# A four-layer graph network on one core: block-ordered loads and stores in fewer transfers, and another order of the first weight loads

## The chip, the cores and the metric

The kernel runs on one core of a Trainium2 chip. The metric is the time of one execution on the device in microseconds (us). Three runs of the kernel before took 5391.73, 5395.11 and 5400.12 us.

The engines are TensorE (PE in the profile, with its weight loads as PEld), VectorE (DVE), ScalarE (ACT), GpSimd (POOL), and SyncE (SP), which here does nothing but issue transfers (DMAs). ACT can issue transfers too.

## What is computed

There are 128 samples. Each is a graph of 128 nodes with 512 features (`x`, 128 x 128 x 512) and a weighted adjacency matrix (`adj`, 128 x 128 x 128). Four layers follow each other, each of the form `x = layernorm(x + layer(x, adj))`, all in float32:

```
# layer 0: attention-weighted diffusion with K = 3 hops
Xw = X @ Wv + bv;  e = leaky_relu(sj[:, None, :] + si[:, :, None] + ab)    # sj, si = Xw @ aw halves
transition = A * exp(e) / sum(A * exp(e));  H = sum_k (Xk @ Wk[k] + bk[k]),  X_{k+1} = transition @ Xk;  relu(H)
# layer 1: two hypergraph convolutions, H = (adj != 0), with relu and layer norm between them
out = D^-1 H B^-1 H^T (x @ W^T) + b                                       # 512 -> 1024, then 1024 -> 512
# layer 2
A = exp(leaky(8 * tanh((s + s^T) / 8))) * adj, rows normalised and rescaled;  out = A @ x @ w
# layer 3: 8-head attention whose scores are multiplied by 2 * adj;  softmax, context, output projection
```

In layer 1 the product `H B^-1 H^T` is one 128 x 128 matrix per sample, called K in the kernel. It is used in both convolutions.

## The kernel before, in words

**Tiling.** Samples go in pairs (`U = 2`), and two pairs go through a layer's stages together. A tile of kind `four` holds a pair's 2 x 512 features for 128 nodes (512 KB); `sq` holds a pair's 128 x 128 matrices (128 KB). All matrix products with weights are done by Strassen's scheme, in layers 0 and 1 and for the attention's q and k twice nested (`twice`, L842; `strassen`, L630). For this the weight blocks and their differences are made once (`prepare0`, L894, for layer 0; the `park_` functions for the later layers, which leave them in DRAM until `take_` brings them in), and sums of blocks of the turned x are made on POOL (`lefts`, L805; `operands`, L615).

**Block order.** A product needs x with features on the partitions. [...] So tiles that are to be turned are loaded in an order of blocks (`from_dram`, L776, for x and adj from the inputs), or go through DRAM and come back in it (`through_dram`, L755). Each of these transfers fills 32 of the 128 partitions, so four make a whole tile. `from_dram` issues four for each sample of a pair: eight transfers of 64 KB for x (runs of 512 bytes), eight of 16 KB for adj (runs of 128 bytes). `turned` (L788) then does the transpose of a tile in one DVE instruction.

`through_dram` has two forms. With `in_order=True` it stores in four transfers, one for each 32 partitions, so that after load and transpose the rows stand in their natural order. With `in_order=False` it stores in one transfer; the rows then come back permuted (row `4 r + m` at place `32 m + r`), and whoever uses them has to undo that. The hidden rows `h` of layer 1 use the first form, with 128 KB per transfer; each sample of a pair is stored by itself.

**Layer 1 around K** (`layer1`, L1172). A pair's adj comes by `from_dram`, is turned, compared with zero on DVE and scaled on POOL. PE multiplies mask and scaled mask into K ("bank<-sq,sq" in the profile). ACT copies K out of PSUM, SP stores it to DRAM in one transfer, and much later, before the second convolution, SP loads it again in one transfer of 130 KB.

**The start** (`prepare0`). The three weights wk of layer 0 (1 MB each) are staged in tiles of `first`. ACT's queue fetches the first column half of all three by row chunks, in loads of 64 KB, and the small vectors (`aw`, `bv`, `bk`, `ab`; those of `aw` and `bv` are read four bytes at a time). The rest comes by SP, after or between the loads of wv (128 KB each) and the first x. ACT then copies the parts into W's blocks, and DVE and POOL form the differences (`combine`, L514; `combine_apart`, L509; `combine_once_more`, L520). DVE also forms `Wv @ aw` by dots of wv's rows with a broadcast `aw` ("junk"); two columns of the blocks B11 and B21 hold the result, so the first products wait for them.

**What sets the order.** All instructions are first recorded in `Plan` (L174) with a key (the stage's place in time, from tables such as `WHEN0`, `WHEN1`, `WHENT`) and with their dependencies. Then `Plan.order` (L239) places them on the five engines one by one, by estimated costs, free buffers and free time; `Plan.deadlines` (L359) gives due times from a first pass, and `Plan.emit` (L370) keeps the best of a few passes and issues everything in that order. Instructions under `plan.together()` stay next to each other. Transfers go round eight semaphore lanes: the ninth waits until the first has landed. [...] Since there is one planner for everything, a change of a few instructions moves others on all engines.

All instructions pass through one line (L381), so the profile tells groups apart by tile names, not by lines. "first" is the large area for the weights of layer 0 and later ones; "bank" and "t" are PSUM; "e" is layer 0's transition matrix on its way through DRAM; "x1d" is x after layer 0.

## Time and profile before

| | |
|---|---|
| median of three runs | 5395.11 us |
| the profiled execution | 5396.67 us |
| its span in the trace | 5394.1 us |
| PE busy in the span | 5308.3 us |
| granted PE clock, mean | 0.996 |
| moved by DMA | 813.71 MB, 151 GB/s |
| transfers issued by SP | 4378, most of them 0.43 us each |

Layer 0 runs from the start to about 1350 us, layer 1 to about 3105 us, layers 2 and 3 to the end. In the rows of groups "x6044 | 1766.2, 434" is the number of instructions, their busy time in us and the mean of one in ns. A product in float32 is two PE instructions. In waits, "16.7, 11, 12.7" is the sum in us, how many, and the longest; the name behind the arrow is what ended the wait by the trace. In a timeline, the first number is the start, the second the length, and several like instructions are merged.

### The profile page before, as it was taken

To read this page: it belongs to the slowest core of one execution; us is meant where nothing else is said; L and a number is where in the kernel's file an instruction comes from. 1 tells how busy PE (TensorE), PEld (TensorE's weight loads), DVE (VectorE), ACT (ScalarE), POOL (GpSimd) and SP (SyncE) were. 2 spreads that over 40 slices of the span, in tenths; PEclk is the share of its full clock that TensorE was granted. 3 is DMA by queue.
4 is the path that set the end of the run, shared out by engine and by line. 5 is a ranking of instruction groups with operands and counts; after the bars stand their busy time and mean duration, and the time that the engine had idled before them with its cause. 6 is when DMAs were issued, how large, how long until landed. Compare 5 with 4: busy or idle time off the path is not lost.

```text
span 5394.1 us, 93993 instructions
## 1 busy us (share of the span) xinstructions
PE 5308.3 (98%) x29039; PEld 4233.2 (78%) x29039; DVE 4436.2 (82%) x11721; ACT 2403.0 (45%) x6085; POOL 3902.7 (72%) x4937
## 2 busy tenths in 40 slices
PE   8999999999999999999999999999999999999998
PEld 4555555555788888888888889888998898888988
DVE  6788888887888888888888878878888888888876
ACT  3334344343444444444444444444444444444444
POOL 6777787675766767676766577777877777778776
PEclk9999999999999999999999999999999999999999
DMA  3444444435554545454554745554555455555543
GB/s 103 133 145 127 143 144 129 132 112 186 147 156 144 161 147 157 148 156 148 156 154 143 246 135 167 154 165 151 164 156 161 153 164 156 163 152 161 160 148 111
DMA packets 842414, 813.71 MB, mean 151 GB/s; under 512 B 269612, under 2 KB 642868, under 8 KB 841912
## 3 DMA queue, kind: packets, MB, share of 16 engines
q1 hardware_dynamic: 838914, 806.65, 49.2%
q8 instruction: 231, 3.78, 0.3%
q14 instruction: 271, 2.22, 0.1%
q10 hardware_dynamic: 2998, 1.06, 0.1%
HBM read 458.38 MB, written 349.04 MB: 150 GB/s over the span
## 4 chain that ended last, share of the span: by engine, by line
PE 88%; DVE 7%; issue 2%; DMA 1%; ACT 1%; POOL 1%; SPq 0%; ACTq 0%; DVEq 0%; POOLq 0%
PE bank L381 69%; PE t L381 20%; DVE out L381 1%; DVE four L381 1%; DVE first L381 1%; DVE col L381 1%; DVE junk L381 1%; SPq L381 0%; DVE side L381 0%; ACT out L381 0%; POOL four L381 0%; DMA four<-x1d 0%; POOL first L381 0%; ACT four L381 0%; DVE rows L381 0%
## 5 line engine op out<-in xcount | busy, mean ns | idle before, releaser
L381 PE MATMUL bank<-first,four 128*128 128x386 f32 (+2 forms) x6044 | 1766.2, 434 | 30.9 <-DVE four L381 15.8
L381 PEld LDWEIGHTS bank<-first,four 128*128 128x128 f32 (+1 forms) x6044 | 1098.5, 190 | 608.8 <-issue 107.7
L381 DVE TENSOR_TENSOR out<-bank,out 128x386 f32<-128x386 f32 (+1 forms) x1999 | 969.9, 504 | 245.3 <-PE bank L381 178.9
L381 POOL TENSOR_TENSOR out<-out 128x772 f32<-128x772 f32 (+2 forms) x262 | 359.1, 1380 | 265.9 <-DVE out L381 188.6
L381 POOL TENSOR_TENSOR four<-four 128x256 f32<-128x256 f32 (+2 forms) x484 | 391.6, 823 | 212.9 <-DVE four L381 153.3
L381 DVE TENSOR_TENSOR four<-bank,four 128x256 f32<-128x256 f32 x1025 | 421.6, 418 | 131.8 <-PE bank L381 122.6
L381 PE MATMUL bank<-first,out 128*128 128x256 f32 x1850 | 458.6, 380 | 1.2 <-DVE four L381 0.6
L381 POOL TENSOR_TENSOR col<-col,neghalf 128x2 f32<-128x2 f32 x320 | 228.8, 715 | 310.9 <-DVE col L381 310.5
L381 ACT COPY out<-bank 128x258 f32<-128x258 f32 (+2 forms) x510 | 204.6, 404 | 544.8 <-PE bank L381 387.9
L381 POOL TENSOR_TENSOR four<-four,four 128x256 f32<-128x256 f32 (+2 forms) x514 | 432.2, 849 | 12.8 <-DVE four L381 5.2
L381 PEld LDWEIGHTS bank<-first,out 128*128 128x128 f32 x1850 | 345.2, 190 | 62.3 <-issue 10.5
L381 ACT ACTIVATE four<-four,col,col 128x512 f32<-128x512 f32 (+1 forms) x314 | 279.6, 914 | 138.7 <-POOL col L381 132.5
L381 DVE TENSOR_TENSOR first<-bank,first 128x256 f32<-128x256 f32 (+1 forms) x601 | 242.7, 416 | 104.4 <-PE bank L381 90.3
L381 PE MATMUL bank<-four,first 128*128 128x128 f32 (+3 forms) x1848 | 292.6, 302 | 1.7 <-DVE out L381 0.9
L381 DVE BATCH_NORM_STATS2 col<-four 128x6 f32<-128x512 f32 x392 | 260.3, 679 | 9.3 <-ACT four L381 8.7
L381 PE MATMUL t<-out,sq 128*128 128x512 f32 x512 | 258.9, 600 | 2.9 <-DVE sq L381 2.5
L381 PEld LDWEIGHTS bank<-four,first 128*128 128x128 f32 (+2 forms) x1848 | 241.7, 186 | 20.1 <-DVE out L381 2.8
L381 PE MATMUL bank<-first 128*128 128x128 f32 (+1 forms) x1972 | 256.0, 277 | 1.5 <-DVE out L381 1.1
L381 PE MATMUL bank<-out,first 128*128 128x128 f32 (+2 forms) x1524 | 251.8, 307 | 4.2 <-ACT side L381 2.2
L381 PEld LDWEIGHTS bank<-first 128*128 128x128 f32 (+1 forms) x1972 | 231.6, 182 | 15.8 <-issue 5.8
L381 PE MATMUL t<-first,four 128*128 128x256 f32 (+2 forms) x1052 | 237.9, 356 | 2.5 <-DVE four L381 1.2
L381 PEld LDWEIGHTS bank<-out,first 128*128 128x128 f32 (+1 forms) x1524 | 207.5, 185 | 27.6 <-issue 8.1
(532 smaller groups left out, 12891.5 us busy)
## 6 DMA issues: line engine op xcount, KB each, us to landing
h<-four SPq DMA_DIRECT2D x312, 128.0 KB, 2.5
four<-in_x_dram SPq DMA_DIRECT2D x504, 64.0 KB, 2.0
four<-in_x_dram SPq DMA_DIRECT2D x61, 512.0 KB, 4.5
x1d<-four SPq DMA_DIRECT2D x61, 512.0 KB, 2.9
out<-x1d SPq DMA_DIRECT2D x51, 512.0 KB, 4.6
first<-S SPq DMA_DIRECT2D x51, 512.0 KB, 4.3
out<-h SPq DMA_DIRECT2D x50, 512.0 KB, 5.3
four<-x1d SPq DMA_DIRECT2D x48, 512.0 KB, 5.2
```

Source lines behind the costliest of these rows:

```text
L381: call(*map(real, args), **{n: real(a) for n, a in kw.items()})
```

## The change

`from_dram` fills 32 partitions for both samples of a pair with one transfer, so four instead of eight per tile: 128 KB each for x and 32 KB for adj. The tile then holds sample j's blocks behind those of sample j - 1, and a new `turned_two` writes the transpose through a pattern with one more dimension. The rows of h are stored with `in_order=False`, in one transfer of 512 KB each. Because they come back permuted, K is loaded again in four transfers that read every fourth row. In `prepare0` wk comes in column halves with all row chunks, in loads of 128 KB: the first halves on ACT's queue, with the small vectors next to the last one, the second halves on SP.

```diff
     def from_dram(src, kind):
 
-        nj, _, n = src.shape
-        t = kind().rearrange("p u f -> p (u f)").rearrange("p (m j w) -> p m j w", m=4, j=nj)
-        for j in range(nj):
-            with plan.together():
-                for k in range(4):
-                    sp.dma_start(t[k * Q:(k + 1) * Q, :, j],
-                                 src[j].rearrange("(m r) (k w) -> k r m w", r=Q, k=4)[k],
-                                 run=n // 4, parts=Q)
-        return t.rearrange("p m j w -> p (m j w)")
+        nj, rows_, n = src.shape
+        w = n // 4
+        t = kind().rearrange("p u f -> p (u f)").rearrange("p (m w) -> p m w", m=4 * nj)
+        with plan.together():
+            for k in range(4):
+                sp.dma_start(t[k * Q:(k + 1) * Q], bass.AP(tensor=src.tensor, offset=src.offset + k * w,
+                                                           ap=[[n, Q], [Q * n, 4 * nj], [1, w]]), run=w, parts=Q)
+        return t.rearrange("p m w -> p (m w)")
...
+    def turned_two(dst, t):
+
+        ve.transpose(dst.rearrange("p (j q) (m r) -> p j m q r", j=U, r=Q),
+                     t.rearrange("p (j m q a) -> p j m q a", j=U, m=4, a=Q))
...
-        def fetch_part(queue, m, chunks, half):
-            at = chunks, slice(half * h, half * h + h)
-            fetch(queue, stage[m][:, at[0], at[1]], wk0[m], *at, h)
...
+        def fetch_half(queue, m, half):
+            columns = slice(half * h, half * h + h)
+            fetch(queue, stage[m][:, :, columns], wk0[m], slice(0, 4), columns, h)
...
-        for m in range(3):
-            fetch_part(ac, m, low, 0)
         awc, bvc = fixed(2 * C, name="aw_c"), fixed(C, name="bv_c")
         ab_b, bk0b = fixed(1, name="ab_b"), row()
-        with plan.together():
-            for c, v, n in ((awc, aw, 2 * C), (bvc, bv0, C)):
-                ac.dma_start(c, bass.AP(tensor=v.tensor, offset=v.offset, ap=[[1, P], [P, n]]), run=1)
-            ac.dma_start(bk0b[:3], bk0, parts=3)
-            ac.dma_start(ab_b, rows(ab, 1), run=1)
         for m in range(3):
-            fetch_part(sp if m else ac, m, high, 0)
+            with plan.together():
+                fetch_half(ac, m, 0)
+                if m == 2:
+                    for c, v, n in ((awc, aw, 2 * C), (bvc, bv0, C)):
+                        ac.dma_start(c, bass.AP(tensor=v.tensor, offset=v.offset, ap=[[1, P], [P, n]]), run=1)
+                    ac.dma_start(bk0b[:3], bk0, parts=3)
+                    ac.dma_start(ab_b, rows(ab, 1), run=1)
...
         plan.key = WHEN0[0] + .05
         for m in range(3):
-            fetch_part(sp, m, every, 1)
+            with plan.together():
+                fetch_half(sp, m, 1)
...
-            turned(xT[-1].rearrange("p u c n -> p (u c) n"), xb)
+            turned_two(xT[-1].rearrange("p u c n -> p (u c) n"), xb)
...
-            turned(AT, ab)
+            turned_two(AT, ab)
...
-            kept.append(part(scratch(f"K{i}", P, U * M), lambda t: t, 0))
-            sp.dma_start(kept[-1], K.rearrange("p b n -> p (b n)"), run=U * M)
+            d = scratch(f"K{i}", P, U * M)
+            kept.append(lambda m, d=d: part(d, lambda t: t.rearrange("(r m) n -> m r n", m=4)[m], 0))
+            sp.dma_start(part(d, lambda t: t, 0), K.rearrange("p b n -> p (b n)"), run=U * M)
...
-                loads.append(through_dram(h[r][b].rearrange("p (j g) (k w) -> p j (g k) w", j=1, k=2), f"h{i + b}"))
+                loads.append(through_dram(h[r][b].rearrange("p (j g) (k w) -> p j (g k) w", j=1, k=2), f"h{i + b}", False))
...
-            sp.dma_start(K.rearrange("p b n -> p (b n)"), kept[r], run=U * M)
+            with plan.together():
+                for m in range(4):
+                    sp.dma_start(K[m * Q:(m + 1) * Q].rearrange("p b n -> p (b n)"), kept[r](m), run=U * M, parts=Q)
```

More of the change, by code (lines that the diff above doesn't have):

```diff
@@ L903, in fetch @@
         def fetch(queue, dst, src, chunks, columns, run):
-            with plan.together():
-                for k in range(4):
-                    queue.dma_start(dst[k * Q:(k + 1) * Q],
-                                    src.rearrange("(k c a) f -> k a c f", k=4, a=Q)[k][:, chunks, columns],
-                                    run=run, parts=Q)
-        def fetch_part(queue, m, chunks, half):
-            at = chunks, slice(half * h, half * h + h)
-            fetch(queue, stage[m][:, at[0], at[1]], wk0[m], *at, h)
@@ L914, in prepare0 @@
-        low, high, every = slice(0, 2), slice(2, 4), slice(0, 4)
-        st = [four() for _ in range(2)]
-        for g, chunks in enumerate((low, high)):
-            plan.key = -9.7 + .2 * g
-            fetch(sp, st[g], wv0, chunks, slice(0, D), D)
+            for k in range(4):
+                queue.dma_start(dst[k * Q:(k + 1) * Q],
+                                src.rearrange("(k c a) f -> k a c f", k=4, a=Q)[k][:, chunks, columns],
+                                run=run, parts=Q)
+        def fetch_half(queue, m, half):
+            columns = slice(half * h, half * h + h)
+            fetch(queue, stage[m][:, :, columns], wk0[m], slice(0, 4), columns, h)
@@ L919, in prepare0 @@
+        st = [four() for _ in range(2)]
+        for g in range(2):
+            plan.key = -9.7 + .2 * g
+            with plan.together():
+                fetch(sp, st[g], wv0, slice(2 * g, 2 * g + 2), slice(0, D), D)
         plan.key = -9
-        for m in range(3):
-            fetch_part(ac, m, low, 0)
         awc, bvc = fixed(2 * C, name="aw_c"), fixed(C, name="bv_c")
         ab_b, bk0b = fixed(1, name="ab_b"), row()
-        with plan.together():
-            for c, v, n in ((awc, aw, 2 * C), (bvc, bv0, C)):
-                ac.dma_start(c, bass.AP(tensor=v.tensor, offset=v.offset, ap=[[1, P], [P, n]]), run=1)
-            ac.dma_start(bk0b[:3], bk0, parts=3)
-            ac.dma_start(ab_b, rows(ab, 1), run=1)
```

## The prediction, made before the changed kernel ran

> **What bounds the kernel now.** I read the page's first part first, then the busy time by stretches of 135 us, then the waits of TensorE (PE) in the stretches that stand out.

> ```profile
> PE 5308.3 (98%) x29039; PEld 4233.2 (78%) x29039; DVE 4436.2 (82%) x11721; ACT 2403.0 (45%) x6085; POOL 3902.7 (72%) x4937
> ...
> 0.00:135.00 135.00, 111.25 (x295) 56.64 (x296) 94.33 (x223) 48.06 (x108) 86.47 (x107) 0.94 0.39 103
> 135.00:270.00 135.00, 134.14 (x408) 72.81 (x407) 105.54 (x274) 53.39 (x120) 100.40 (x123) 1.00 0.45 133
> ...
> 1215.00:1350.00 135.00, 123.64 (x396) 69.46 (x394) 97.99 (x278) 49.72 (x109) 73.23 (x95) 0.96 0.57 186
> 1350.00:1485.00 135.00, 130.05 (x620) 108.04 (x621) 115.31 (x329) 66.76 (x110) 95.30 (x140) 0.97 0.50 145
> ...
> 5265.00:5400.00 135.00, 115.73 (x861) 103.07 (x860) 85.63 (x213) 60.77 (x205) 84.20 (x95) 0.96 0.31 102
> ```

> The columns are the stretch, its length, then the busy time of PE, weight loads, DVE, ACT and POOL, the granted clock, the DMA share and GB/s. PE is busy 5308 of 5394 us. Of the 86 us in which it idles, 24 lie in the first stretch, 11 + 5 around 1350 (where layer 0 ends and layer 1 begins), 13 in the last 129 us. A stretch in the middle of a layer loses 0.3 to 1 us. So nothing that shortens DMA or SP work in mid-layer can pay; only the start, the change of layer and the tail can.

> ```profile
> PE bank L381 <- DVE four L381: 12.7, 1, 12.7
> ...
> PE bank L381 <- POOL sq L381: 10.0, 1, 10.0
> PE t L381 <- DVE sq L381: 2.5, 1, 2.5
> ```

> The first line is the first 60 us: PE waits for the turned x. The other two are 1200 to 1400: one wait of 10 us for a mask operand, one of 2.5 us for a turned transition matrix. What SP issued before each:

> ```profile
> 14.21 4.45 SPq L381 DMA_DIRECT2D first<-in_L_gnn_Wk_dram  x8
> 18.70 3.74 SPq L381 DMA_DIRECT2D four<-in_x_dram  x8
> 22.49 5.65 SPq L381 DMA_DIRECT2D first<-in_L_gnn_Wk_dram  x12
> ...
> 1339.22 4.70 SPq L381 DMA_DIRECT2D e<-sq  x8
> 1343.97 3.75 SPq L381 DMA_DIRECT2D sq<-in_adj_dram  x8
> ```

> SP issues back to back, one transfer per 0.47 us, from 14 to 28 us. At 1343.97 it issues the adj load that the 10 us wait is for, behind eight stores of e.

> [...] the clock is 0.50 from 40 to 50 us, and after the 10 us wait four t products take 3.43 us where they take 1.88. So each long wait costs more than its length. [...] Here the x blocks of 64 KB land in 2.0 us and the wv loads of 128 KB in 2.8, so 128 KB per issue moves more per issue. [...] The row of 128x1024 transposes shows 1236 ns.

> **The change, part by part.**

> (1) Fewer issues. Loads of x go from 8 to 4 per pair (64 pairs, -256), adj blocks likewise (-256), h stores from 8 to 2 per pair (-384), K loads from 1 to 4 (+192), wk on SP from 20 to 12 (-8): -712 of 4378. At 0.43 us that is 306 us less of SP's queue. Bytes and run lengths stay. In mid-layer this hides under PE: worth 0. The h store's one issue saves about 3 x 0.43 us before its reload, also under PE. K's last piece is issued 3 x 0.43 = 1.3 us later, and in the trace nobody waited for K's load: 0.

> (2) Transposes. Same elements, same 32-element runs, but a pattern with one more dimension (2x4x4x32 for 4x8x32). Not in the trace. From below: no reason for a gain. From above: twice the time, 64 x 1.24 = 79 us of DVE in layer 0 and 64 x 0.43 = 28 in layer 1. I take 0[...].

> (3) The start. In the changed built order SP issues x of the first pair (4), wv (8), x of the second pair (4), then the 12 second halves of wk. The last of these is place 27 of the queue; it was 45. That is 18 x 0.47 = 8.5 us of issue, but the bytes do not shrink: 0.5 + 1.0 + 0.5 + 1.5 MB on SP and 1.5 MB on ACT's queue are 5.0 MB. At 218 GB/s (the stretch from 5 to 10 us) they need 23 us from 2.9, so they land near 26 where the old last half was issued at 28.1 and landed near 31. PE's first product does not come earlier. It needs whole column halves of all three wk (3.0 MB with x and wv, landing at about 15 to 16.7), then ACT's copies, then on DVE one subtraction (0.56), the transpose (1.24) and four dots (4 x 0.76 = 3.0, with the read of the accumulator), then ACT's small copy: about 22 to 24, against 22.44. On ACT's queue the 4-byte loads of aw and bv now stand behind four wk loads; whatever they delay is in that span. What does come earlier is the second pair's transpose, at 31.92 before. In the changed order, from DVE's first subtraction (16.5 to 18.4) to that transpose stand 4 subtractions, 1 transpose, 8 dots, 3 short adds and 2 more subtractions, 6 x 0.56 + 1.24 + 8 x 0.76 + 3 x 0.28 = 11.5 us: 28 to 30. POOL's sums, and the combinations for wk's second half (POOL at 40.6 before), follow it 2 to 4 us earlier. I take **-3 us** for the start; both ends are +3 (wk's halves late) and -8 (a half-clock stretch at 40 to 50 goes too).

> (4) The change of layer. Idle at 1325 to 1385: 0.62 + 0.52 + 2.54 + 10.05 + 0.74 + 0.46 + 0.46 = 15.4 us. Half clock after the two long waits: (3.78 - 1.88) + (1.06 - 0.59) + (1.38 - 0.61) + (3.43 - 1.88) = 4.7. Sum 20.1. In the changed order the third pair's adj load is whole (4 issues), right behind the reload of an e, ahead of the seven w2 loads and of the last e stores; before, half of it stood behind them. I put it at about 1318. Landing takes 5 us under the weight loads (DMA share 1.0 there), then DVE and POOL 5 us each, so the operand stands at 1328 to 1332. PE reaches that product after 15.6 us of listed work from the first mask product (1311.7), near 1327.6. A wait of up to 5 us, with half clock up to 2.3, remains; the 2.8 us of short waits stay. The last e is then queued on SP behind the third K store, hence behind this product: e stores 1333.9 to 1337.6, fourth adj load to 1339.5, both usable by 1344 to 1350; PE has 41 rows of products (18 us) to do in between and wants them at 1350. What is late next is thus this pair, with little to spare. Gain 20.1 - 5 - 2.3 - 2.8 = **-10 us**; ends 0 (the wait only moves) and -17.

> (5) Everything else is reordered, since one planner places all instructions. PE's mid-layer idle is 0.3 to 1 us in 135; I take 0, with +-3. The tail keeps its order in kind: 0.

> Sum: -3 - 10 = -13. The profiled execution took 5396.67 us for its span of 5394.1, and it is 1.6 above the median of the three runs; on the median, 5395.11 - 13 = 5382.

> **Rivals.**

> (A) The wait moves. The last e, its adj load and the third K store are one chain on SP; if the third product is late by more than the 6 us of slack above, PE stops at the e product instead, and the start's gain is all that stays: 5395 - 3 = 5392. For it: POOL is busy 8.3 of 10 us at 1340 to 1350, so sums may be late anyway. Against it: 41 rows stand in between where there were 11.

> (B) The transposes cost more, on the slower side. Place: DVE in layer 0, busy about 113 of 135 us. Price: up to 79 us of DVE, of which a half would delay the adds that PE waits for: 39, less the 13 gained, so about 5421. It decides from the point where more than 24 us are not covered (13 + 10.8), which is an extra 0.37 us per transpose uncovered. For it: the pattern is not in the trace. Against it: [...] DVE's 22 idle us per stretch.

> (C) The change does nothing on the path, since DMA issue is hidden in all of mid-layer and the start is bound by bytes: 5395 +- 4.

> **How the numbers follow.** About 0.2%, or 10.8 us, is what a measurement of this kernel can tell from no change. Forecast 0.56, with its own range 5370 to 5386; A 0.22, C 0.09, B 0.09; 0.04 for reorderings in mid-layer of either sign. Of the forecast's share about 0.06 lies above 5384.3. Faster: 0.50 + 0.02 = 0.52. Same: 0.22 + 0.09 + 0.06 = 0.37. Slower: 0.09 + 0.02 = 0.11. The range reaches from both parts at their best with the reordering's 3 (5395 - 8 - 17 - 3 = 5367) over A and C with its 4 to about 5398 (5395 + 3); B and half of the 0.04 lie outside.

> **What would show it.** Right: SP's wk halves issued by about 21 us, the second pair's transpose before 30; the 10 us wait for POOL's sq near 1343 gone or below 5; PE idle in the 1215 and 1350 stretches down from 16 to about 8; 128x1024 transposes still at 1.24 us. Wrong: a new wait above 5 us on the t product of the last e (A); transposes in layer 0 above 1.6 us (B); a first product after 25 us; or mid-layer stretches that lose more than 1.5 us each, which nothing above explains.

## The result, and the profile after

The changed kernel took 5384.96 us (median of 15 runs, 5380.15 to 5390.55), the kernel before 5396.36 (15 runs). The ratio is 0.9979, 95% interval 0.9971 to 0.9987: 11 us faster, where 13 were forecast. Its profiled execution took 5387.95 us with a span of 5386.2, so 8 us less than the one before; this execution lies 3 us above its kernel's median. The sum was close. The experiments below show that its terms were not.

The page's first part, then the busy time by stretches (columns as above), both of the changed kernel:

```profile
PE 5310.0 (99%) x29039; PEld 4227.9 (78%) x29039; DVE 4421.4 (82%) x11721; ACT 2407.3 (45%) x6085; POOL 3903.9 (72%) x4937
```

```profile
0.00:135.00 135.00, 112.12 (x308) 56.77 (x309) 96.61 (x238) 50.00 (x113) 89.07 (x112) 1.00 0.47 108
...
1215.00:1350.00 135.00, 132.24 (x455) 77.90 (x453) 103.22 (x293) 53.57 (x116) 80.88 (x109) 1.00 0.59 189
1350.00:1485.00 135.00, 132.44 (x636) 109.28 (x635) 121.11 (x349) 71.20 (x115) 98.65 (x140) 1.00 0.52 169
2970.00:3105.00 135.00, 130.19 (x650) 109.32 (x649) 101.96 (x275) 51.12 (x101) 72.26 (x96) 0.99 0.67 222
```

PE's idle time around 1350 fell from 16.3 to 5.3 us, and the clock there is 1.00. The first stretch idles about as long as before. Its clock reads 1.00 instead of 0.94, since the half clock that the kernel before had from 39.6 to 53.2 us is gone. (The trace records the clock only from 32.3 us on here, and from 25.9 in the kernel before. Earlier, PE was slower than that 1.00 says: in the changed kernel the first four products at 25.20 took 2.94 us, while four of the same shape took 1.56 in the kernel before at 31.46.) The last line is the change from layer 1 to 2: 4.8 us idle. There the kernel before had 0.8, and 4.3 in the stretch after it, where the changed one has 2.9.

PE's waits of the changed kernel, in the first 60 us and then from 1200 to 1400:

```profile
PE bank L381 <- DMA row<-in_L_gnn_bk_dram: 9.2, 1, 9.2
PE bank L381 <- ACT first L381: 8.5, 1, 8.5
```

```profile
PE bank L381 <- DVE four L381: 1.0, 2, 0.6
PE bank L381 <- ACT four L381: 0.9, 2, 0.5
```

The 10.0 and 2.5 us waits of the change of layer are gone. At the start, PE first waits for a small vector that is now issued behind four wk loads; what it then computes ends at 16.73, and DVE's dots begin only at 21.99. The wait that counts is the next one, now for a copy by ACT, not for the turned x. What SP issued at both places:

```profile
1.13 1.82 SPq L381 DMA_DIRECT2D four<-in_x_dram  x4
5.99 6.75 SPq L381 DMA_DIRECT2D four<-in_L_gnn_Wv_dram  x8
13.53 3.01 SPq L381 DMA_DIRECT2D four<-in_x_dram  x4
16.59 6.67 SPq L381 DMA_DIRECT2D first<-in_L_gnn_Wk_dram  x12
...
1319.95 1.91 SPq L381 DMA_DIRECT2D sq<-in_adj_dram  x4
1321.90 0.96 SPq L381 DMA_DIRECT2D four<-in_x_dram  x2
1322.91 3.32 SPq L381 DMA_DIRECT2D first<-w2s  x6
...
1334.43 8.57 SPq L381 DMA_DIRECT2D e<-sq  x8
1343.10 1.85 SPq L381 DMA_DIRECT2D sq<-in_adj_dram  x4
```

The third pair's adj is loaded whole at 1319.95, ahead of the w2 loads, as the built order said. PE's third mask product begins at 1329.61 without a wait, though only just: POOL finished its operand at 1329.30.

### The profile page after: what moved, and what is told of

Same layout as the page of the kernel before. It is cut to its first block, busy times and chain, and to the rows that moved or that the text cites. A ratio compares the mean times of both kernels' runs of the same rounds, so it can differ in the third digit from the quotient of the medians.

```text
span 5386.2 us, 92938 instructions
## 1 busy us (share of the span) xinstructions
PE 5310.0 (99%) x29039; PEld 4227.9 (78%) x29039; DVE 4421.4 (82%) x11721; ACT 2407.3 (45%) x6085; POOL 3903.9 (72%) x4937
## 3 DMA queue, kind: packets, MB, share of 16 engines
q8 instruction: 231, 3.78, 0.3%
## 4 chain that ended last, share of the span: by engine, by line
PE 87%; DVE 7%; issue 2%; DMA 2%; POOL 1%; ACT 1%; SPq 0%; DVEq 0%; ACTq 0%; POOLq 0%
PE bank L381 66%; PE t L381 21%; DVE four L381 2%; DVE out L381 1%; DVE col L381 1%; DVE junk L381 1%; DVE first L381 1%; POOL four L381 0%; POOL out L381 0%; DMA four<-x 0%; ACT out L381 0%; ACT four L381 0%; DMA four<-in_x_dram 0%; DVE rows L381 0%; DMA first<-in_L_gnn_Wk_dram 0%
## 5 line engine op out<-in xcount | busy, mean ns | idle before, releaser
L381 PE MATMUL bank<-first,four 128*128 128x386 f32 (+3 forms) x6352 | 1747.5, 422 | 21.7 <-ACT first L381 8.5
L381 PEld LDWEIGHTS bank<-first,four 128*128 128x128 f32 (+2 forms) x6352 | 1087.7, 186 | 600.0 <-DVE out L381 105.3
L381 DVE TENSOR_TENSOR out<-bank,out 128x386 f32<-128x386 f32 (+1 forms) x1942 | 948.6, 507 | 251.0 <-PE bank L381 197.2
L381 DVE TENSOR_TENSOR four<-bank,four 128x256 f32<-128x256 f32 x1113 | 453.8, 416 | 151.9 <-PE bank L381 140.0
L381 POOL TENSOR_TENSOR out<-out 128x772 f32<-128x772 f32 (+3 forms) x249 | 341.7, 1382 | 263.7 <-DVE out L381 202.9
L381 POOL TENSOR_TENSOR four<-four 128x256 f32<-128x256 f32 (+2 forms) x434 | 350.0, 819 | 197.3 <-DVE four L381 135.9
L381 PE MATMUL bank<-first,out 128*128 128x256 f32 (+1 forms) x1746 | 434.1, 379 | 3.7 <-DVE four L381 1.6
L381 POOL TENSOR_TENSOR four<-four,four 128x256 f32<-128x256 f32 (+2 forms) x467 | 396.6, 854 | 10.1 <-PE bank L381 1.9
L381 POOL TENSOR_TENSOR col<-col,neghalf 128x2 f32<-128x2 f32 x320 | 227.4, 711 | 224.3 <-DVE col L381 222.9
L381 ACT COPY out<-bank 128x258 f32<-128x258 f32 (+2 forms) x489 | 194.8, 404 | 434.3 <-PE bank L381 355.1
L381 PEld LDWEIGHTS bank<-first,out 128*128 128x128 f32 (+1 forms) x1746 | 319.4, 189 | 66.0 <-issue 9.0
L381 ACT ACTIVATE four<-four,col,col 128x512 f32<-128x512 f32 (+1 forms) x355 | 307.9, 892 | 125.2 <-POOL col L381 122.9
L381 DVE TENSOR_TENSOR first<-bank,first 128x256 f32<-128x256 f32 (+1 forms) x591 | 240.6, 416 | 97.8 <-PE bank L381 89.0
L381 PE MATMUL bank<-first 128*128 128x128 f32 (+1 forms) x2132 | 297.7, 277 | 1.6 <-DVE four L381 1.6
L381 DVE BATCH_NORM_STATS2 col<-four 128x6 f32<-128x512 f32 x424 | 283.0, 681 | 10.6 <-ACT four L381 9.1
L381 ACT COPY four<-bank 128x256 f32<-128x256 f32 (+1 forms) x358 | 150.6, 424 | 302.2 <-PE bank L381 282.4
L381 PEld LDWEIGHTS bank<-first 128*128 128x128 f32 (+1 forms) x2132 | 270.0, 190 | 16.0 <-issue 3.9
L381 ACT COPY t<-out 128x512 f32<-128x512 f32 x256 | 151.0, 591 | 241.3 <-PE bank L381 100.8
L381 PE MATMUL t<-out,sq 128*128 128x512 f32 x512 | 256.3, 594 | 0.5 <-ACT t L381 0.5
L381 PE MATMUL t<-first,four 128*128 128x256 f32 (+2 forms) x1064 | 250.2, 361 | 0.6 <-DVE four L381 0.6
L381 PE MATMUL bank<-out,first 128*128 128x128 f32 (+3 forms) x1432 | 232.5, 312 | 2.2 <-DVE col L381 1.8
L381 PE MATMUL bank<-four,first 128*128 128x128 f32 (+3 forms) x1400 | 220.6, 303 | 4.1 <-DVE first L381 1.4
```

Of the source, the lines that this page charges most:

```text
L381: call(*map(real, args), **{n: real(a) for n, a in kw.items()})
```

## The experiments

My first theory (T) was the prediction's: the gain lies at the change of layer 0 to 1, by the place of one adj load, and the rest is small. Its rivals were that the start carries the gain (S), that the fewer h issues do (H), and later that the number of issues around that place counts, not the place (F).

All twelve experiments beside the kernel before, which took 5394 to 5398 us (medians of 17 to 31 runs on the chips concerned). The first four rows come from one chip, the rows that begin with p_ from a second, the others from a third. The kernel before differs by up to 4 us between these, so that differences of this size between rows from different chips say nothing; there the ratios are the better guide:

| kernel | median us (range) | ratio to before, 95% |
|---|---|---|
| a_blocks: block loads alone | 5361.1 (5358.8 to 5361.6) | 0.9931 (0.9918 to 0.9943) |
| b_hk: h and K alone | 5401.5 (5398.6 to 5407.4) | 1.0009 (1.0001 to 1.0017) |
| c_start: wk's start alone | 5396.2 (5392.5 to 5403.4) | 0.9997 (0.9989 to 1.0005) |
| d_nostart: all but wk's start | 5377.3 (5374.9 to 5382.0) | 0.9962 (0.9950 to 0.9975) |
| a_h: block loads and one h store | 5377.8 (5377.5 to 5379.3) | 0.9969 (0.9957 to 0.9980) |
| a_k: block loads and K in four | 5360.0 (5357.7 to 5362.4) | 0.9936 (0.9922 to 0.9949) |
| after_again: the change once more | 5383.4 (5378.6 to 5391.8) | 0.9981 (0.9974 to 0.9987) |
| g_whole: eight issues kept together | 5382.0 (5380.0 to 5385.7) | 0.9979 (0.9970 to 0.9987) |
| p_one_as_four: as d_nostart, planned as four | 5358.0 (5357.4 to 5359.6) | 0.9926 (0.9914 to 0.9939) |
| p_four_as_one: as a_k, planned as one | 5388.8 (5383.1 to 5391.6) | 0.9981 (0.9974 to 0.9989) |
| p_after_as_four: the change, planned as four | 5365.2 (5364.1 to 5368.1) | 0.9940 (0.9928 to 0.9953) |
| t_third: one load of before changed | 5392.0 (5389.1 to 5395.6) | 0.9995 (0.9986 to 1.0003) |

To see where each kernel's time goes, I gave each product the median interval between equal products in the trace of before. These sum to 5186.3 us of work in every kernel. What the times of the trace show beyond that is lost time. Lost us by stretches of work, from the one profiled execution of each. Two executions of one program (changed and after_again) differ by 1.9 us at the start, by 3.5 in layers 2 and 3, by 1.2 in the tail and by 0.2 at most elsewhere, so smaller differences than these aren't read:

```
us of work:       0-135  -1250  -1400  -2900  -2980  -3240  -5000  -5186    sum
                  start layer0 change layer1 itsend change lay2,3   tail
before             37.4   24.2   23.9    9.8    1.9   14.1   69.3   27.2  207.8
t_third            36.8   24.1   17.2   10.1    2.1   15.5   70.2   27.8  203.9
b_hk               37.9   24.2   23.7   18.6    6.5   12.0   64.9   25.5  213.2
c_start            39.1   28.3   20.5    9.9    1.9   14.7   64.9   26.1  205.5
changed            32.5   26.1    9.9   11.6    8.3   13.6   70.8   27.0  199.8
after_again        34.4   26.0   10.1   11.7    8.3   13.4   67.3   25.8  197.0
p_four_as_one      30.7   24.4   11.0   15.4    7.0   14.2   69.5   25.4  197.7
d_nostart          32.5   23.4    9.7   11.9    6.5   12.6   65.6   26.9  189.1
a_h                30.9   22.0   10.0   12.3    8.2   12.8   67.2   25.9  189.3
p_after_as_four    34.9   25.6   10.2    8.8    3.0   11.4   57.4   24.9  176.3
g_whole            32.1   36.3   19.2   10.9    2.8   12.0   57.6   24.6  195.5
a_blocks           31.6   22.6   10.4    9.8    2.7   12.9   59.4   24.0  173.5
a_k                32.3   22.8   11.7    9.1    3.1   11.4   59.3   24.5  174.3
p_one_as_four      32.9   22.2   10.2    8.8    3.0   11.5   57.3   25.1  171.1
```

### The parts by themselves

a_blocks takes only the new `from_dram` and `turned_two`. b_hk takes only `in_order=False` for h and the four K loads. c_start takes only `prepare0`. d_nostart is the changed kernel with the old `prepare0`. Each is before with those hunks of the diff above and no others:

```diff
 # a_blocks                      # b_hk
+turned_two(..., xb)             +through_dram(h..., f"h{i + b}", False)
+turned_two(AT, ab)              +for m in range(4): sp.dma_start(K[m * Q:(m + 1) * Q]..., kept[r](m), ...)
 # c_start                       # d_nostart: a_blocks and b_hk together
+fetch_half(ac, m, 0)
+fetch_half(sp, m, 1)
```

> The kernel before with only the block loads of the change: x and adj of two samples in one set of four transfers and one 4-dim transpose; h stores, K loads and wk's start as before. Theory T (the gain lies at the change from layer 0 to 1, because the third pair's adj load is now whole and stands ahead of the seven w2 loads): the built order there is the changed kernel's, so the 10 us wait near 1343 and its half clock are gone, PE idle of the stretches at 1215 and 1350 together falls from 16 to about 5 to 7 us, and the time is 5396 - 10 = about 5386 (5383 to 5390). Rival S (the gain comes from the start, wk in column halves): this kernel keeps wk's old start but for four x issues fewer ahead of it, so at most -3, 5393 to 5397, with the transition's gain given back later. Transposes stay at 1.23 to 1.24 us in both.

> The kernel before with only h in one store and K loaded in four pieces. The built order still has half of the third pair's adj load behind two w2 loads and half of w2 behind it. Theory T: the 10 us wait near 1343 stays, the mid-layer issues are hidden, 5396 within 3. Rival H (fewer h issues, 384 of the 712 removed, let reloads come earlier and carry part of the gain): 5388 to 5392, seen as less idle in the stretches from 1350 on and not at 1343.

> The kernel before with only the start of the change: wk fetched by column halves, 12 transfers on ACT's queue and 12 on SP's, wv and x beside it; x still in 8 issues per pair. Theory T: the first product is later (25 us as in the changed kernel or up to 2 us more, since SP issues 8 more x transfers ahead of the second wk halves), the half clock from 40 to 55 us is gone or shorter, at work of 135 us the loss is about 5 us less than before, 2 to 3 of which are given back by 600 us; the 10 us wait near 1343 stays because the third pair's adj load is in halves: 5391 to 5394. Rival S (the start carries the whole gain): 5385 within 3.

> The changed kernel with the wk fetch of before (row halves at first, ACT and SP mixed), block loads, h and K as changed. Theory T: no long wait at the change of layer; only the start's part is lost, so 2 to 5 us above the changed kernel: 5387 to 5390. Rival S: the whole gain is lost, 5394 to 5397. Third case (start and transition overlap because what is gained at the start is given back at 430 to 540 us of work anyway): the same time as the changed kernel within 1.5.

All four came out outside every range that was given for them. Theory T named the right part and missed its size. The block loads alone gain 36 us, three times the whole change. h and K alone lose a little (interval above 1). wk's start alone is worth nothing that can be told from zero. With h and K added the 36 become 20 (d_nostart), and with wk's start they become 11. So the change holds one gain and two losses.

In the table, the block loads explain the start (37.4 to 31.6) and the change of layer (23.9 to 10.4), as d_nostart and the changed kernel show too. But a_blocks also loses 10 us less in layers 2 and 3, whose code the change doesn't touch. Compared product by product from the end, the last 15,242 of PE's 29,039 products have the same shapes in the changed kernel as in before. a_blocks agrees for the last 324, and for 94 of 100 of those 15,242. The planner found another order there. Nothing in the block loads aims at it, so these 10 of the 36 us are luck.

### Which of h and K costs 16 us

```diff
 # a_h: a_blocks with
-  loads.append(through_dram(h[r][b].rearrange(...), f"h{i + b}"))
+  loads.append(through_dram(h[r][b].rearrange(...), f"h{i + b}", False))
 # a_k: a_blocks with K in four loads of straight rows
-  sp.dma_start(K.rearrange("p b n -> p (b n)"), kept[r], run=U * M)
+  for m in range(4):
+      sp.dma_start(K[m * Q:(m + 1) * Q].rearrange("p b n -> p (b n)"), kept[r](m), run=U * M, parts=Q)
```

> Block loads as changed, plus h in one store per sample; K loaded in one piece as before, so the rows of h meet K in another order than the reference has (nothing is left out). The block loads alone took 5361; with h and K both changed it was 5377. Theory K (K's load in four pieces is the 16 us: its last piece is 1.3 us later at each of 64 places): this kernel stays at 5361 within 3. Theory H (the one h store is the 16 us, by the order that the planner then finds in layer 1's end and in layers 2 and 3): 5374 to 5380, with the waits of 1.5 and 2.5 us at the end of layer 1 back and layers 2 and 3 in the order of the kernel before.

> Block loads as changed, plus K loaded in four pieces of straight rows; h in four stores as before. Theory K: 5374 to 5380. Theory H: 5361 within 3. If the 16 us come from no single part but from which order the planner happens to find, neither of the two kernels need match: then each one's loss in layers 2 and 3 goes with its order there, not with its edit.

> The changed kernel once more, beside the others of this call. Its median was 5385.0 and that of the same kernel with wk's start of before 5377.3. If wk's column halves cost what the profiles of the two show in layer 0 (2.8 us at the end of layer 0), this is 5380 to 5383; if the medians are right, 5385 within 2.

K costs nothing (5360.0 against 5361.1). The h store is the 16 us, as theory H said, and a_h has before's order in layers 2 and 3. PE's waits from 2960 to 3100, first of a_h, then of a_blocks:

```profile
PE t L381 <- DVE junk L381: 2.3, 2, 1.5
PE t L381 <- DVE four L381: 1.1, 1, 1.1
```

```profile
PE bank L381 <- DVE out L381: 1.8, 2, 1.0
PE t L381 <- DVE four L381: 0.6, 2, 0.3
```

With one h store, PE waits for DVE's dots ("junk") at the end of layer 1, up to 1.5 us at a time; the changed kernel has the same two waits, and a_blocks has none for dots. The changed kernel repeated its time within 1.6 us, so that wk's new start seems to cost the 6 to 8 us between it and d_nostart. Their ranges still overlap a little; the pair p_one_as_four and p_after_as_four below, on one chip, shows it with ranges apart.

### The store, or the order that comes with it

The planner was given a count of issues that differs from the one executed: `as_if` multiplies the estimated time and the lanes of a transfer in `Plan` and does nothing else.

```diff
 # p_one_as_four (d_nostart) and p_after_as_four (changed kernel): one h store, planned as four
-  sp.dma_start(part(d, ...), src[:, j], run=nw)
+  sp.dma_start(part(d, ...), src[:, j], run=nw, as_if=4 if name[0] == "h" else 1)
 # p_four_as_one (a_k): four h stores, planned as one
-  src[m * Q:(m + 1) * Q, j], run=nw, parts=Q)
+  src[m * Q:(m + 1) * Q, j], run=nw, parts=Q, as_if=.25 if name[0] == "h" else 1)
```

> Block loads, h in one store and K in four loads as changed, wk's start of before; but the planner is told to count the one h store as four issues, so every engine gets the order that it has with four h stores (the order of the kernel that took 5360), and only one transfer is issued where that one issues four. Theory O (what the one h store costs, 16 us, is only the order that the planner finds with it): 5360 within 3. Theory D (the one store itself is slower: all of h lands later and the reload with it): 5374 to 5380, with waits for turned h in layer 1.

> The reverse: block loads and K in four pieces, h in four stores, wk's start of before, but the planner counts the four h stores as one issue, so the order is that of the kernel with one h store (5377). Theory O: 5377 within 3, with the waits of 1.5 and 1.1 us at the end of layer 1 and 65 to 67 us lost between 3240 and 5000 us of work. Theory D: 5360 within 3. If SP's three more issues per sample hurt in an order that did not count them: above 5380.

> The changed kernel whole, wk's column halves too, with the one h store counted as four issues by the planner. Theory O: the changed kernel's 5384 less the 16 us that the order costs, 5365 to 5371; what then still separates it from 5360 is the price of wk's new start (some 6 us). Theory D: 5384 within 3. If wk's start costs only through the order that the planner finds after it, this is 5358 to 5362.

Theory O holds. p_one_as_four issues what d_nostart issues, in the order of a_k, and takes 5358.0 instead of 5377.3; it is the fastest kernel of the study. In the traces its 29,039 products have the shapes of a_k's one by one, and those of p_four_as_one have d_nostart's. p_four_as_one shows the last case of its expectation as well: in the order made for one store, three more issues per sample cost another 11 us (5388.8 against 5377.3). Its profiled execution shows 3.5 of them in layer 1, where h is stored; where the rest lies stays open. p_after_as_four gives the changed kernel the other order and gains 18 to 20 us; the 7 that still separate it from p_one_as_four are wk's.

Layers 2 and 3 lost 64.9 to 70.8 us in the nine executions with before's order there, and 57.3 to 59.4 in the five with the other. PE's busy time in one stretch of layer 3, first of a_blocks, then of the changed kernel:

```profile
3645.00:3780.00 135.00, 134.56 (x997) 122.91 (x996) 108.93 (x284) 62.27 (x217) 104.85 (x128) 1.00 0.52 161
```

```profile
3645.00:3780.00 135.00, 134.13 (x989) 120.63 (x988) 108.43 (x277) 60.10 (x198) 102.86 (x130) 1.00 0.52 161
```

It is 0.4 us in 135, over and over. PE's waits from 3300 to 5000 us show what it is made of, first of a_blocks, then of the changed kernel:

```profile
PE bank L381 <- DVE rows L381: 3.2, 14, 0.3
PE bank L381 <- DVE first L381: 2.0, 9, 0.2
PE bank L381 <- DVE out L381: 1.5, 1, 1.5
```

```profile
PE bank L381 <- DVE col L381: 3.2, 15, 0.3
PE bank L381 <- DVE four L381: 2.7, 12, 0.3
PE t L381 <- DVE col L381: 1.6, 8, 0.2
PE t L381 <- DVE out L381: 1.4, 6, 0.2
```

In these traces the median time from a product of 256 columns to the next one is 0.22 us. Up to about 5100 us, 50 to 54 of them in these layers are followed only after 0.4 us or more in the nine executions, and 25 or 26 in the five. Beyond the median, these cost 19 to 21 us against 10 to 11. So the 8 to 10 us are some 26 short waits of PE for DVE that the other order doesn't have. In each of the nine, 25 of the waits are for "col", in the five none. Why the planner finds one order or the other stays open.

### The change of layer: the place of one load, or the number of issues

```diff
 # g_whole: before, with the eight issues of a block load kept together
-        for j in range(nj):
-            with plan.together():
+        with plan.together():
+            for j in range(nj):
                 for k in range(4):
 # t_third: before, with the new load and transpose for one pair of layer 1
-  from_dram(adj[i:i + U], sq)
+  (from_dram_two if i == 4 else from_dram)(adj[i:i + U], sq)
```

> The kernel before with one edit: the eight issues of a pair's block load are kept together instead of four and four; as many issues, the same bytes and transposes. In the built order the third pair's adj load is then whole and ahead of the seven w2 loads; at the start the second pair's x stands behind all of wk. Theory T (place of that load, not the number of issues): the 10 us wait near 1343 and its half clock are gone, -14 at the change of layer; the start is 0 to +4 worse: 5382 to 5388. Rival F (fewer issues are what count, since SP is busy without a gap there): the wait stays at over 5 us, 5393 to 5400.

> The kernel before with one load of its 128 changed: the adj block of layer 1's third pair comes in four issues instead of eight, with its 4-dim transpose. In the built order it is now whole where its first half stood (SP at about 1332 us), no longer split by the last eight e stores; layers 2 and 3 keep the order of the kernel before. Theory T (the 10 us wait is that this one load is split by the e stores): its operand stands at about 1345 instead of 1352.8, the wait falls from 10 to 2 or 3 us and most of its half clock goes; the loss from 1250 to 1400 us of work falls from 24 to 14 to 17, and nothing else moves: 5387 to 5390 against about 5397. Rival F (SP is late there because every pair takes eight issues, and the other loads keep that): the wait moves to the next pair or the last e, as in the kernel that kept eight issues together; 19 to 24 us stay lost there: 5392 to 5398.

g_whole came out at the edge of theory T's range for the wrong reason. Its 10 us wait is gone, but the change of layer still loses 19.2 us and layer 0 loses 12 more than before. Its gain of 12 us is the size of what the other order in layers 2 and 3 saves (69.3 to 57.6); the rest cancels. At the change of layer a new wait came up, for POOL's sums. t_third removed part of the wait without touching any other load. PE of g_whole, then of t_third, from 1325 on (start, length, products merged, idle before and what ended it):

```profile
1332.49 0.70 PE L381 MATMUL bank<-first,side 128*128 128x256 f32 x2 [2.40 <-POOL side L381]
...
1336.44 3.60 PE L381 MATMUL t<-out,sq 128*128 128x512 f32 x4
```

```profile
1330.69 1.99 PE L381 MATMUL t<-out,sq 128*128 128x512 f32 x4 [1.90 <-DVE sq L381]
...
1343.26 1.38 PE L381 MATMUL bank<-sq,sq 128*128 128x130 f32 x4 [4.05 <-POOL sq L381]
```

The wait for the third pair's mask fell from 10.05 to 4.05 us and the stretch from 23.9 to 17.2. The run's time agrees in sign, but at 5392.0 it lies at the edge of rival F's range, and its interval contains 1. So both theories hold in part, by one trace: 7 of the 14 us come from this one load's being unsplit, and keeping eight issues together is not enough. That the other 7 come from the shorter loads of the other pairs is what remains; no kernel tested it by itself.

## Why the prediction was right, and where it was not

The likeliest case happened (faster, near the bound of 0.2%), and 5385.0 is 3 us from 5382. That it came so close is partly luck: in the traces gains of 19 us stand against a loss of 11, where 13 and 0 were forecast. By its steps:

**(1) Fewer issues in mid-layer, worth 0.** Right for K's load (a_k) and for the issues themselves: in one and the same order, one h store instead of four changed 5360.0 to 5358.0, with overlapping ranges. But in an order that wasn't made for them, three issues more per sample cost 11 us (p_four_as_one against d_nostart). "Hidden under PE" is true of an order, not of an issue.

**(2) Transposes at no extra cost.** The 0 was an estimate that no trace had shown, and it came out right; rival B is out. The largest group of the changed kernel has a mean of 1231 ns where 1236 was shown. It holds transposes with the old pattern too; in layer 0 alone, where the new pattern stands, the 68 transposes of this size took 1230 ns on average and 1242 at most (1236 and 1248 before):

```profile
L381 DVE STREAM_TRANSPOSE four<-four 128x1024 f32<-128x1024 f32 x107 | 131.7, 1231 | 5.4 <-DMA four<-x 5.2 <-DMA four<-h 0.2
```

**(3) The start, -3.** The sum came out at -4.9 (37.4 to 32.5), but its cause was wrong. wk's column halves were to bring the second pair forward; they hold it back. The block loads do bring it forward, to 25.11 in a_blocks. The first product came at 25.20 (forecast 22 to 24, "wrong" above 25), the second pair's transpose at 31.18 (28 to 30), the last wk issue at 23.3 (21; its place in SP's queue is 29, not 27). c_start, which has them alone, gains nothing at the start (39.1); a_blocks gains 5.8 without them. ACT's timeline of the changed kernel shows the term that was mis-sized, then a_blocks' of the same span, then the first products of the changed kernel and of a_blocks:

```profile
7.36 7.29 ACTq L381 DMA_DIRECT2D first<-in_L_gnn_Wk_dram  x8
14.67 1.28 ACT L381 ACT_TABLE_LOAD   x1 [14.67 <-DMA first<-in_L_gnn_Wk_dram]
15.97 0.62 ACT L381 COPY first<-first 128x512 f32<-128x512 f32 x1
...
18.73 1.14 ACT L381 COPY first<-first 128x512 f32<-128x512 f32 x2 [0.32 <-DMA first<-in_L_gnn_Wk_dram]
19.78 0.89 ACT L381 COPY t<-first 128x386 f32<-128x386 f32 x2
```

```profile
2.87 6.57 ACTq L381 DMA_DIRECT2D first<-in_L_gnn_Wk_dram  x12
9.53 1.28 ACT L381 ACT_TABLE_LOAD   x1 [9.53 <-DMA first<-in_L_gnn_Wk_dram]
10.82 1.27 ACT L381 COPY first<-first 128x512 f32<-128x512 f32 x2
...
13.58 0.62 ACT L381 COPY first<-first 128x512 f32<-128x512 f32 x1 [1.49 <-DMA first<-in_L_gnn_Wk_dram]
14.24 0.90 ACT L381 COPY t<-first 128x386 f32<-128x386 f32 x2
```

```profile
25.20 2.94 PE L381 MATMUL bank<-first,four 128*128 128x386 f32 x4 [8.46 <-ACT first L381]
```

```profile
19.67 2.94 PE L381 MATMUL bank<-first,four 128*128 128x386 f32 x4 [9.87 <-ACT first L381]
```

From the copies to t to the first product both kernels take 5.4 us, so the delay arises before them. The prediction put wk's landing at 15 to 16.7. The last load of the first halves was issued at 14.32 and landed at 18.55, and the two copies that needed it began at 18.73. In a_blocks the copies to t need only the first rows of each wk (twelve loads of 64 KB instead of twelve of 128), and their last copy could begin at 13.58. The last load was issued so late because the transfers waited for their semaphore lanes, eight in this trace: the last one's lane was free at 14.30, when an earlier transfer had landed. The eight loads held ACT for 7.29 us, of which the issues themselves take 2.8. One of these waits, from 7.69 to 8.94, was for aw's four-byte load (landed at 8.92), which the prediction named but gave no price of its own. In both timelines ACT's table load stands right behind its last issue (at 14.67 and at 9.53), and its first copy behind that. So the first copy moved from 10.82 to 15.97. In the end it didn't decide, since ACT still had to wait for the landing at 18.73 (in c_start by 1.37 us). Of the 5.5 us that the first product is late, 1 to 3 are left at 135 us of work (32.5 and 34.4 against 31.6), hardly more than the two executions of the changed kernel differ by; in between, the changed kernel's clock stays at 1.00 from 40 to 50 us, where a_blocks has 0.69. Another 3.5 us go in layer 0 (26.1 against 22.6).

**(4) The change of layer, -10.** Right in place and mechanism, too small: -14.0 (23.9 to 9.9). The wait of up to 5 us and 2.3 of half clock that were kept as remainder did not come. The load was issued at 1319.95 and its operand stood at 1329.30, within the forecast 1328 to 1332, but PE came to it only at 1329.61, 17.4 us after its first mask product (1312.20) and not 15.6 (which from 1311.7 gives 1327.3, not 1327.6). The last e's product was not late either (1351.95), so rival A is out, though narrowly: its store took 8.57 us of SP, not 3.7, and DVE finished turning that e at 1351.77.

**(5) Everything else, 0 with 3 either way.** This is the step that failed, in size: +11 in the profile. Layer 0 lost 1.9 us more (one stretch of it, 405 to 540 us, idles 2.2, one of the prediction's own signs of being wrong), layer 1 1.8, its end 6.4, the rest about 1 together. The end of layer 1 is the order that comes with one h store, shown by p_one_as_four (3.0 where d_nostart has 6.5). Its larger effect was invisible in the comparison of before and after: both have the same order in layers 2 and 3, so that the 8 us of the other order, which the block loads alone obtain, appear in neither. Rival C is out as well: the path did move, by -19 and +11.

## What to carry to other kernels

Where a planner orders all instructions, test every part of a change alone and also in the order of its neighbour: the same transfers in another order differed by 19 us, more than the change was worth. The transfers here share eight semaphore lanes, and the last of ACT's twelve wk loads was issued at 14.32, when an earlier transfer had landed (14.30), and landed itself at 18.55: reckon the landing of a group from its last issue, not from the bytes alone. A load that is split by other work is whole only with its last part: in the kernel before, the two halves of the third pair's adj were issued from 1331.78 and from 1343.97, and PE waited 10.05 us. So look for what stands between the issues.

## What the runs showed of the hardware

Two waits of about 2.5 us came with half clock: after one of 2.54 us (before) four t products took 3.78 us, where they take 1.88 at a clock of 1.00, and after one of 2.40 (g_whole) 3.60. But the length of a wait alone doesn't decide. After 1.90 us in t_third four t products took 1.99; in the changed kernel the clock halved at 5165.97 after a wait of 1.80 us (ended at 5164.49). A wait of 1.28 us near the end was followed by half clock in the kernel before (from 5347.28) and not in the changed kernel, where it ended at 5338.43.
